# One convolution tap moved from VectorE to ScalarE and GpSimd in a Mamba and FFN block on one core

## The chip, the cores and the metric

The kernel runs on one core of a Trainium2 chip. The metric is the device time of one execution in microseconds; the time before is 591.6 us, the median of three runs (589.13 to 591.79). Besides these there is one profiled execution, from which all views of the profile come.

The names of the engines in the views: PE is TensorE (matmuls; PEld are its weight loads), DVE is VectorE, ACT is ScalarE, POOL is GpSimd, SP is SyncE, which here only issues DMAs.

## The reference

Four sequences of 512 tokens with 256 features go through a Mamba layer and then through an FFN. Both are modulated by a small vector per sequence. Cut to what matters here:

```python
h = _layernorm(x) * (1 + ca) + sa
proj = h @ W_in.T
xBC, z, A_log = split(proj, [CONV_DIM, CONV_DIM + D_INNER])    # 4352, 256, 32 columns
xc = conv_general_dilated(xBC, conv_w, padding=(3, 0), groups=CONV_DIM)
xBC = xc + conv_b                       # causal, 4 taps, each channel for itself
x, B, C = split(xBC, [256, 256 + 2048])  # 32 heads: x 8 wide, B and C 64 wide
a = -softplus(A_log)
Lm = exp(segsum(a))                     # decay from token s to token l, per head
y = (C @ B.T * Lm) @ x + D * x          # per head
x = x + ga * (y * silu(z + z_bias) @ W_out.T)
h = _layernorm(x) * (1 + cb) + sb
x = x + gb * (fwht(silu(h @ W1.T) * (h @ W3.T)) @ W2.T)
```

A channel's convolution is out[l] = b + w3 v[l] + w2 v[l-1] + w1 v[l-2] + w0 v[l-3], where v is a projected channel along the tokens.

## The kernel before

Channels or tokens lie on the 128 partitions, 512 tokens along the free dimension. A sequence is cut into eight chunks of 64 tokens: within a chunk, heads attend by matmuls (`attend`, `intra`); from chunk to chunk, states are handed on (`states`, `turn_states`, `inter`).

**Steps.** The Mamba layer is done in 64 steps k (`NP = 64`), eight for each of eight units n, a unit being half of the heads (i) of one sequence (b). Step k projects 128 channels of B (`bc`, half 0) and 128 of C (`cc`, half 1) with six matmuls each into one PSUM bank (`project`, `proj`, L244), and convolves each (`conv`). Each unit also projects and convolves 128 channels of x (`x_proj`). That makes 64 + 64 + 8 convolutions.

**A convolution** (`conv`, L387 to L394): ACT writes the tap w3 with the bias to `dst` and, in a second pass over the bank, w0 times the bank to a buffer `cv` of three; DVE adds tap w2 (L392) and tap w1 (L393), both read from the bank; POOL, which does not touch the bank, adds `cv`, shifted by three tokens (L394). The framework orders the accesses of different engines to a bank in the order in which the program states them. Three banks (`ps_p`) take turns for the projections.

**Around it.** `attend(k)`, for odd k, multiplies bc and cc of k - 1 and k in 128 small matmuls and weights the results by the decays `lt` (L460, DVE). `turn_b` turns bc with PE and copies it with ACT (L468). A unit's decays from chunk to chunk are made by `x_decays`: ACT takes the exponential of `de` into `dx` (L489), DVE sets the first column to zero (L491), and ACT spreads it eightfold to `dc` (L493), 1024 columns, which the scans over the chunks read in `turn_states` (L561). `turn_states` ends with a masked copy by POOL (`sts`, L565). `x_part2` copies the convolved x twice side by side into `xd`, in two halves of 256 tokens (L507, ACT); `x_part3` turns them with PE (L515) and spreads them for the later matmuls. `xd` and the scans' result `sn` share one pair of buffers (tag "xd").

**Order.** The order of the instructions of each engine is fixed when the program is built. The steps are put in an agenda, and each piece of work is called at its due time, counted in steps: `project` at k - 1.11 and k - 1, `prep_l` at k - 1.31, `attend` at k + 0.12, `x_proj` at 8n + 1.32, `x_part1` (which calls `x_decays`) at 8n + 2.12, `x_part2` at 8n + 3.46, `x_part3` at 8n + 3.77; `turn_states(m)` at 4m + 5.47, two for each unit. A planner with an estimate of every instruction's duration then takes, for each engine but SP, what is ready, by that priority. SP's DMAs stay in the order of the agenda, and each waits on SP until its data and its buffer are there; those behind it wait too. `load_d` at 4m - 3.13 fetches decays for `prep_l`, `x_fetch` at 8n - 1.5 (1.2 for n = 0) fetches `ex` and `de`, `write_sums` writes what they read, and `load_x`, `refill`, `fetch` and the spills move activations and weights. From step 60 on the FFN of the finished sequences begins (`ffn_up`, `ffn_down`).

Of the kernel before, what the change touches and what calls it, by code (L numbers as in the profile page):

```python
# [16 lines left out]
AF = mybir.ActivationFunctionType  # L17
ALU = mybir.AluOpType
# [3 lines left out]
NB, S, DM = 4, 512, 256  # L22
NH, HD = 32, 8
Q = 64
NC = S // Q
# [5 lines left out]
def mamba_ffn(tc, ctx, u, c_t, wmod, win_t, cw, cb, zb, dsk, wo_t, w13_t, w2_t,  # L31
              k_ident, k_reset, k_dl, k_dr, k_had, k_own, out):
    nc = tc.nc
    ve, ac, gp, pe = nc.vector, nc.scalar, nc.gpsimd, nc.tensor
# [14 lines left out]
    def at_time(t, fn, *args):  # L49
        heappush(agenda, (t, next(ids), fn, args))  # L50
# [9 lines left out]
    def work(shape, name, tag, bufs=2, dtype=F32):  # L60
        return wk.tile(shape, dtype, name=name, tag=tag, bufs=bufs)
# [4 lines left out]
    def ptile(name):  # L66
        return ps_p.tile([128, S], F32, name=name, tag="p")
# [174 lines left out]
    def proj(ps, w, c0, ht):  # L242
        for n, (a, b, k) in enumerate(TERMS):
            last[pe] = pe.matmul(ps, w[:, a, k, c0 : c0 + 128], ht[k][:, b], start=(n == 0), stop=(n == 5))  # L244

    last = {}
# [137 lines left out]
            nc.sync.dma_start(p_dr[b][:, 128 * t : 128 * t + 128], phs[32 * t : 32 * t + 32])  # L384
            nc.sync.dma_start(p_end[b][:, 2 * t : 2 * t + 2], phs[32 * t : 32 * t + 32, Q - 1 :: Q])

    def conv(ps, tl, dst):  # L387
        w = cw_sb[:, tl]
        ac.activation(dst, ps, AF.Identity, bias=cb_sb[:, tl : tl + 1], scale=w[:, 3:4])  # L389
        v = work([128, S], "cv", "cv", 3)  # L390
        last[ac] = ac.activation(v, ps, AF.Copy, scale=w[:, 0:1])  # L391
        ve.scalar_tensor_tensor(dst[:, 1:], ps[:, : S - 1], w[:, 2:3], dst[:, 1:], ALU.mult, ALU.add)  # L392
        last["conv"] = ve.scalar_tensor_tensor(dst[:, 2:], ps[:, : S - 2], w[:, 1:2], dst[:, 2:], ALU.mult, ALU.add)  # L393
        last[gp] = gp.tensor_tensor(dst[:, 3:], dst[:, 3:], v[:, : S - 3], ALU.add)  # L394

    units = [(i, b) for i in range(2) for b in range(NB)]
    NP = 64
# [3 lines left out]
    T = dict(  # L401
        attend=0.12, turn_b=0.13, prep_l=-1.31, proj_b=-1.11, proj_c=-1, load_d=-3.13,
        states=-0.03, intra=0.1, turn=1.47, inter=2.53,
        x_proj=1.32, x0=-1.5, x1=2.12, x2=3.46, x3=3.77, gate_z=5.89, fin0=3.54, fin1=3.96, fin2=4.99, fin3=6.63,
        pro0=-11.83, pro1=-7.06, pro2=-4.93, pro3=-4.48, pro4=-3.88, next_ht=-3.77, pro04=0.27,
        quads=1.55, xz1=32.3, wo=19.68, mod=18.99, w2=40.89, wf0=56.74, wf1=62.02, wf2=62.29,
        load_w2=63.01, w2tag=1, w2gp=0, p3gp=1, first_h2=59.14, lag=4.89, next_h2=-2.27,
    )

    def where(k):  # L410
        i, b = units[k // 8]
        return i, b, (k // 4) % 2, k % 4
# [21 lines left out]
    def project(k, half):  # L434
        i, b, pp, g = where(k)
        w = wq[2 * i + pp]
        tl = 2 + 8 * (2 * i + pp) + 2 * g
        dct, nm, nb = ((bcs, "bc", 3), (ccs, "cc", 8))[half]
        pb = ptile(f"p{nm}{k}")
        proj(pb, w, 256 * g + 128 * half, ht[i, b])  # L440
        dct[k] = work([128, S], f"{nm}{k}", nm, nb)
        conv(pb, tl + half, dct[k])

    def attend(k):

# [33 lines left out]
    def x_part1(n):  # L479

        with behind(ac):
            x_decays(n)

    def x_decays(n):
        ex = exs[n]
        ac.activation(ex, ex, AF.Exp)

        de = work([128, 16, NC], f"dx{n}", "dx", 1)
        ac.activation(de.rearrange("p (a g j) c -> p a g (j c)", a=2, g=4),  # L489
                      des.pop(n).rearrange("p (g a j) c -> p a g (j c)", a=2, g=4), AF.Exp)  # L490
        ve.memset(de[:, :, 0:1], 0.0)  # L491
        dc = dcs[n] = work([128, 16, HD, NC], f"dc{n}", "dc", 1)
        ac.activation(dc, de.unsqueeze(2).to_broadcast([128, 16, HD, NC]), AF.Copy)  # L493

    def x_proj(n):
        i, b = units[n]
        px = ptile(f"px{n}")
        proj(px, wxz[i], 0, ht[i, b])
        xcs[n] = work([128, S], f"xc{n}", "xc")
        conv(px, i, xcs[n])  # L500

    def x_part2(n):
        xds[n] = []
        for hf in range(2):
            xd = work([128, 4, 2, Q], f"xd{n}{hf}", "xd", 2)
            xch = xcs[n][:, 256 * hf : 256 * hf + 256].rearrange("p (c l) -> p c l", l=Q)
            ac.activation(xd, xch.unsqueeze(2).to_broadcast([128, 4, 2, Q]), AF.Copy)  # L507
            xds[n].append(xd)

    def x_part3(n):  # L510
# [162 lines left out]
    for k in range(AHEAD):  # L673
        for half in range(2):
            with behind(pe, ve):
                project(k, half)
        if k == 1:
            with behind(gp, ac):
                split_quad(1, 0, q10)
# [46 lines left out]
    hid, pds, x2, gb = {}, {}, {}, {}  # L726
# [48 lines left out]
    for k in range(NP):  # L775
        if k % 2:
            at_time(k + T["attend"], attend, k)
        at_time(k + T["turn_b"], turn_b, k)
        if k >= AHEAD:
            at_time(k + T["proj_b"], project, k, 0)  # L780
            at_time(k + T["proj_c"], project, k, 1)
        if k >= LOOK_P:
            at_time(k + T["prep_l"], prep_l, k)
    for n, (i, b) in enumerate(units):
        if n:
            at_time(8 * n + T["x_proj"], x_proj, n)
        at_time(8 * n + T["x0"] if n else 1.2, x_fetch, n)
        if i == 0 and n > 1:
            at_time(8 * n + T["pro0"] - 2.5, preload, b)
        at_time(8 * n + T["x1"], x_part1, n)  # L790
        at_time(8 * n + T["x2"], x_part2, n)
        at_time(8 * n + T["x3"], x_part3, n)
        at_time(8 * n + T["gate_z"], gate_z, n)
        for part in range(4):
            at_time(8 * n + 8 + T[f"fin{part}"], finish_unit, n, part)
        if n and i == 0:
            for part in range(5):
                at_time(8 * n + T[f"pro{part}"], prologue, b, part)
        if i == 1:
            at_time(8 * n + T["next_ht"], next_ht, b)  # L800
# [89 lines left out]
```

## Time and profile before

| what | us |
|---|---|
| median of the runs | 591.6 |
| the profiled execution | 590.94 |
| its span, from first to last instruction | 588.7 |
| PE busy | 543.6 (92% of the span) |
| PE weight loads busy | 433.2 (74%) |
| DVE busy | 405.1 (69%) |
| ACT busy | 390.5 (66%) |
| POOL busy | 328.0 (56%) |
| POOL's L394, 64 of bc and 64 of cc | 70.1 + 69.8 |
| DVE's L392 and L393 of bc and cc | 47.5 + 47.5 + 47.6 + 47.4 |
| ACT's L389 and L391 of bc and cc | 50.1 + 50.2 + 44.3 + 44.1 |
| ACT's L507, 16 copies to `xd` | 10.3 |
| ACT's L493, 8 copies to `dc` | 8.7 |
| packets of the SP queue: share of 16 DMA engines | 27.2% |

A row of the page's groups reads: line, engine, operation, out<-in by the program's names, shapes, count, then busy us in all and the mean ns of one, then the engine's idle time just before them and what ended most of it. A row of waits reads: who waited, for whom, us in total, how many times, the longest. The span is less than the time of the execution by what lies around the instructions. The busy time of an engine is an average over two stages, the Mamba layer and the FFN, in which different engines are loaded, so the stages have to be looked at apart.

### The profile page before, as it was taken

To read this page: it belongs to the slowest core of one execution; us is meant where nothing else is said; L and a number is where in the kernel's file an instruction comes from. 1 tells how busy PE (TensorE), PEld (TensorE's weight loads), DVE (VectorE), ACT (ScalarE), POOL (GpSimd) and SP (SyncE) were. 2 spreads that over 40 slices of the span, in tenths; PEclk is the share of its full clock that TensorE was granted. 3 is DMA by queue.
4 is the path that set the end of the run, shared out by engine and by line. 5 is a ranking of instruction groups with operands and counts; after the bars stand their busy time and mean duration, and the time that the engine had idled before them with its cause. 6 is when DMAs were issued, how large, how long until landed. Compare 5 with 4: busy or idle time off the path is not lost.

```text
span 588.7 us, 16269 instructions
## 1 busy us (share of the span) xinstructions
PE 543.6 (92%) x6836; PEld 433.2 (74%) x6836; DVE 405.1 (69%) x683; ACT 390.5 (66%) x654; POOL 328.0 (56%) x301
## 2 busy tenths in 40 slices
PE   3698999899899999999999999889989999999996
PEld 3566786677677766777776767667767898888886
DVE  5967878988876776889786878687855454343243
ACT  6889789798965978887795776768674243232321
POOL 5673447445553578466465556467666655334341
PEclk9998999999998999999999899999989999999999
DMA  6423201123012353015003142154148036204021
GB/s 192 124 77 137 70 2 73 26 55 108 18 32 87 114 149 115 3 61 171 7 4 112 76 131 83 60 157 162 37 145 296 2 117 183 77 0 153 1 80 37
DMA packets 42112, 52.00 MB, mean 88 GB/s; under 512 B 18230, under 2 KB 30260, under 8 KB 42040
## 3 DMA queue, kind: packets, MB, share of 16 engines
q1 hardware_dynamic: 40504, 50.54, 27.2%
q8 instruction: 54, 0.88, 0.6%
q10 hardware_dynamic: 1472, 0.38, 0.3%
q14 instruction: 18, 0.15, 0.1%
q0 software_dynamic: 64, 0.05, 0.0%
HBM read 33.51 MB, written 17.44 MB: 87 GB/s over the span
## 4 chain that ended last, share of the span: by engine, by line
PE 40%; DVE 5%; DMA 3%; ACT 2%; issue 2%; POOL 2%; POOLq 0%; DVEq 0%
PE f L244 15%; PE pdy L712 4%; PE pdyi L712 4%; PE pcc L244 4%; PE pbc L244 3%; PE po L612 2%; DMA w2a<-w_t 2%; PE pG L257 1%; PE py L548 1%; PE pi L574 1%; PE bT L466 1%; PE ps L532 1%; DVE sn L561 1%; DMA wf<-w_t 1%; PE px L244 1%
## 5 line engine op out<-in xcount | busy, mean ns | idle before, releaser
L394 POOL TENSOR_TENSOR bc<-bc,cv 128x509 f32<-128x509 f32 x64 | 70.1, 1095 | 58.6 <-DVE bc L393 41.0
L394 POOL TENSOR_TENSOR cc<-cc,cv 128x509 f32<-128x509 f32 x64 | 69.8, 1091 | 56.5 <-DVE cc L393 40.3
L244 PE MATMUL f<-h,wf 128*128 128x512 f32 x384 | 97.6, 395 | 0.0
L244 PEld LDWEIGHTS f<-h,wf 128*128 128x128 f32 x384 | 69.2, 190 | 12.4
L705 POOL TENSOR_TENSOR fl<-ft,fh 128x512 fp32r<-128x512 f32 x31 | 40.1, 1295 | 56.8 <-ACT fh L704 52.0
L392 DVE SCALAR_TENSOR_TENSOR cc<-pcc,cw_sb,cc 128x511 f32<-128x511 f32 x64 | 47.5, 743 | 28.9 <-ACT cv L391 28.9
L389 ACT ACTIVATE bc<-pbc,cb_sb,cw_sb 128x512 f32<-128x512 f32 x64 | 50.1, 783 | 22.8 <-PE pG L257 15.7
L389 ACT ACTIVATE cc<-pcc,cb_sb,cw_sb 128x512 f32<-128x512 f32 x64 | 50.2, 785 | 21.2 <-PE pcc L244 15.6
L244 PE MATMUL pcc<-ht,wq 128*128 128x512 f32 x192 | 53.6, 412 | 6.6 <-DVE dx L491 3.0
L704 ACT ACTIVATE fh<-ft 128x512 fp32r<-128x512 f32 x32 | 20.2, 631 | 58.5 <-DVE ft L701 29.5
L700 DVE SCALAR_TENSOR_TENSOR ft<-ft,f 128x512 f32<-128x512 f32 x32 | 21.9, 687 | 51.5 <-ACT ft L699 49.3
L244 PE MATMUL pcc<-hr,wq 128*128 128x512 f32 x192 | 53.9, 414 | 2.8 <-DVE bc L393 1.9
L392 DVE SCALAR_TENSOR_TENSOR bc<-pbc,cw_sb,bc 128x511 f32<-128x511 f32 x64 | 47.5, 742 | 11.1 <-ACT cv L391 11.0
L244 PE MATMUL pbc<-ht,wq 128*128 128x512 f32 x192 | 54.1, 417 | 0.0
L244 PE MATMUL pbc<-hr,wq 128*128 128x512 f32 x192 | 52.2, 405 | 1.9 <-DVE cc L393 1.8
L393 DVE SCALAR_TENSOR_TENSOR bc<-pbc,cw_sb,bc 128x510 f32<-128x510 f32 x64 | 47.6, 743 | 1.4
L393 DVE SCALAR_TENSOR_TENSOR cc<-pcc,cw_sb,cc 128x510 f32<-128x510 f32 x64 | 47.4, 741 | 1.1
L244 PEld LDWEIGHTS pcc<-ht,wq 128*128 128x128 f32 x192 | 35.5, 193 | 16.4 <-ACT cv L391 3.9
L460 DVE TENSOR_TENSOR l<-pG,l 128x512 f32<-128x512 f32 x64 | 41.0, 681 | 6.7 <-PE pG L257 6.5
L468 ACT ACTIVATE bt<-bT 128x512 f32<-128x512 f32 x64 | 38.8, 606 | 9.9 <-PE bT L466 9.7
L391 ACT ACTIVATE cv<-pbc,cw_sb 128x512 f32<-128x512 f32 x64 | 44.3, 692 | 1.4 <-POOL cc L394 1.4
L391 ACT ACTIVATE cv<-pcc,cw_sb 128x512 f32<-128x512 f32 x64 | 44.1, 690 | 0.0
(152 smaller groups left out, 1231.0 us busy)
## 6 DMA issues: line engine op xcount, KB each, us to landing
wq<-win_t SPq DMA_DIRECT2D x16, 256.0 KB
htd<-ht SPq DMA_DIRECT2D x8, 512.0 KB
hr<-htd SPq DMA_DIRECT2D x8, 512.0 KB
h2d<-ht SPq DMA_DIRECT2D x8, 512.0 KB
h<-h2d SPq DMA_DIRECT2D x8, 512.0 KB
x<-u SPq DMA_DIRECT2D x7, 512.0 KB
ex<-pd SPq DMA_DIRECT2D x8, 256.0 KB
ygd<-yg SPq DMA_DIRECT2D x4, 512.0 KB
```

Of the source, the lines that this page charges most:

```text
L244: last[pe] = pe.matmul(ps, w[:, a, k, c0 : c0 + 128], ht[k][:, b], start=(n == 0), stop=(n == 5))
L389: ac.activation(dst, ps, AF.Identity, bias=cb_sb[:, tl : tl + 1], scale=w[:, 3:4])
L391: last[ac] = ac.activation(v, ps, AF.Copy, scale=w[:, 0:1])
L392: ve.scalar_tensor_tensor(dst[:, 1:], ps[:, : S - 1], w[:, 2:3], dst[:, 1:], ALU.mult, ALU.add)
L393: last["conv"] = ve.scalar_tensor_tensor(dst[:, 2:], ps[:, : S - 2], w[:, 1:2], dst[:, 2:], ALU.mult, ALU.add)
L394: last[gp] = gp.tensor_tensor(dst[:, 3:], dst[:, 3:], v[:, : S - 3], ALU.add)
L460: ve.tensor_tensor(lts[n], pg, lts[n], ALU.mult)
L468: ac.activation(bts[k], pt, AF.Copy)
L700: ve.scalar_tensor_tensor(t, t, 1.0, p1, ALU.add, ALU.mult)
L704: ac.activation(hi, t, AF.Copy)
L705: (ve if (b, f) == (NB - 1, 7) else gp).tensor_tensor(lo, t, hi.bitcast(F32), ALU.subtract)
L712: last[pe] = pe.matmul(pds[t // 2][:, t % 2], hid[a][:, tok], w2h[f][:, w_], start=(f == 0 and t % 2 == 0 and m == 0), stop=(f == 7 and m ...
```

## The change

Five edits:

- For even k, the convolution of `cc` is `shared`: DVE makes only tap w2. ACT makes a third pass over the bank, w1 times the bank to a new buffer `cv1` of two. POOL adds `cv`, shifted by one, to `cv1`, and then adds `cv1`, shifted by two, to `dst`. The other convolutions stay as they are.
- `dc` is spread by POOL.
- `xd` is filled by DMA from SBUF to SBUF, two DMAs for each half of the tokens, four for a unit, all issued by SP.
- `x_part2` is due at 8n + 2.6 in place of 8n + 3.46.
- For n = 0 it is due at 0.6, ahead of `load_d(1)` (0.87), `write_sums` (1.0) and `x_fetch(0)` (1.2).

```diff
-    def conv(ps, tl, dst):
+    def conv(ps, tl, dst, shared=False):
         w = cw_sb[:, tl]
         ac.activation(dst, ps, AF.Identity, bias=cb_sb[:, tl : tl + 1], scale=w[:, 3:4])
         v = work([128, S], "cv", "cv", 3)
         last[ac] = ac.activation(v, ps, AF.Copy, scale=w[:, 0:1])
         ve.scalar_tensor_tensor(dst[:, 1:], ps[:, : S - 1], w[:, 2:3], dst[:, 1:], ALU.mult, ALU.add)
-        last["conv"] = ve.scalar_tensor_tensor(dst[:, 2:], ps[:, : S - 2], w[:, 1:2], dst[:, 2:], ALU.mult, ALU.add)
-        last[gp] = gp.tensor_tensor(dst[:, 3:], dst[:, 3:], v[:, : S - 3], ALU.add)
+        if shared:
+
+            v1 = work([128, S], "cv1", "cv1", 2)
+            ac.activation(v1, ps, AF.Copy, scale=w[:, 1:2])
+            gp.tensor_tensor(v1[:, 1:], v1[:, 1:], v[:, : S - 1], ALU.add)
+            last[gp] = gp.tensor_tensor(dst[:, 2:], dst[:, 2:], v1[:, : S - 2], ALU.add)
+        else:
+            last["conv"] = ve.scalar_tensor_tensor(dst[:, 2:], ps[:, : S - 2], w[:, 1:2], dst[:, 2:], ALU.mult, ALU.add)
+            last[gp] = gp.tensor_tensor(dst[:, 3:], dst[:, 3:], v[:, : S - 3], ALU.add)
...
-        x_proj=1.32, x0=-1.5, x1=2.12, x2=3.46, x3=3.77, gate_z=5.89, fin0=3.54, fin1=3.96, fin2=4.99, fin3=6.63,
+        x_proj=1.32, x0=-1.5, x1=2.12, x2=2.6, x3=3.77, gate_z=5.89, fin0=3.54, fin1=3.96, fin2=4.99, fin3=6.63,
...
-        conv(pb, tl + half, dct[k])
+        conv(pb, tl + half, dct[k], k % 2 == 0 and half == 1)
...
-        ac.activation(dc, de.unsqueeze(2).to_broadcast([128, 16, HD, NC]), AF.Copy)
+        gp.tensor_copy(dc, de.unsqueeze(2).to_broadcast([128, 16, HD, NC]))
...
-            ac.activation(xd, xch.unsqueeze(2).to_broadcast([128, 4, 2, Q]), AF.Copy)
+            for r in range(2):
+                nc.sync.dma_start(xd[:, :, r], xch)
...
-        at_time(8 * n + T["x2"], x_part2, n)
+        at_time(8 * n + (T["x2"] if n else 0.6), x_part2, n)
```

## The prediction

> **What bounds the kernel now.** I read the page's busy table and slices first, then the windows, then the waits of TensorE (PE) inside the window that matters, then single stretches of the timeline. The mamba stage fills about 30 to 440 us, the FFN stage the rest. The windows view of these two (length; then busy us of PE, PEld, DVE, ACT, POOL):
>
> ```profile
> 30.00:440.00 410.00, 383.91 (x5745) 294.21 (x5745) 321.94 (x542) 322.36 (x548) 242.15 (x222) 0.98 0.26 81
> 440.00:588.00 148.00, 143.38 (x1018) 125.74 (x1016) 60.92 (x98) 46.07 (x76) 67.19 (x55) 1.00 0.29 96
> ```
>
> The reader is to see that in the first stage no engine is saturated: PE is busy 94%, VectorE (DVE) and ScalarE (ACT) 79% each, GpSimd (POOL) 59%. The convolutions lie wholly in that stage. PE's idle time there is 410 - 383.9 = 26.1 us. Some time is lost inside its busy time too; the page's groups show it:
>
> ```profile
> L244 PE MATMUL f<-h,wf 128*128 128x512 f32 x384 | 97.6, 395 | 0.0
> L244 PE MATMUL pcc<-ht,wq 128*128 128x512 f32 x192 | 53.6, 412 | 6.6 <-DVE dx L491 3.0
> L244 PE MATMUL pcc<-hr,wq 128*128 128x512 f32 x192 | 53.9, 414 | 2.8 <-DVE bc L393 1.9
> L244 PE MATMUL pbc<-ht,wq 128*128 128x512 f32 x192 | 54.1, 417 | 0.0
> L244 PE MATMUL pbc<-hr,wq 128*128 128x512 f32 x192 | 52.2, 405 | 1.9 <-DVE cc L393 1.8
> ```
>
> The same 512-column matmul costs 97.6/384 = 254 ns in the FFN stage and 213.8/768 = 278 ns in the mamba stage, where the stream is interrupted: 24 ns x 768 = 18.6 us. I count 26.1 + 18.6 = 44.7 us as PE's lost time. The waits view of PE for 30 to 440 us (total, times, longest) says who ended it:
>
> ```profile
> PE pcc L244 <- DVE bc L393: 3.3, 5, 1.2
> PE xt L515 <- DVE l L460: 3.0, 4, 1.2
> PE pcc L244 <- DVE dx L491: 3.0, 3, 2.5
> PE pt L292 <- ACT bt L468: 2.5, 2, 1.6
> PE pcc L244 <- ACT cv L391: 2.2, 2, 1.1
> PE pl L430 <- DMA dr<-p: 2.1, 1, 2.1
> PE pbc L244 <- DVE cc L393: 1.8, 2, 1.2
> PE bT L466 <- ACT bt L468: 1.6, 3, 0.7
> PE pl L430 <- DVE sn L561: 1.3, 2, 0.8
> ```
>
> The rows below these hold 0.2 to 1.2 us each. All rows by releaser: DVE 14.9, ACT 7.5, DMA 2.1, POOL 0.8, together 25.3. So DVE ends 59% of PE's waits, ACT 30%, POOL 3%; laid over 44.7 us that is 26.3, 13.3 and 1.4 us.
>
> **What the Trainium skill says.** "PSUM — Partial Sum Buffer", section "PSUM bank collisions raise a hardware error", says that any two engines on one bank and quadrant must be kept apart, two readers included. The trace agrees: the first DVE tap needs only what L389 wrote, yet it starts after ACT's second read of the same bank (L392 on cc waits for cv L391, 28.9 us in 24 waits). "DMA: Bandwidth & Descriptors", section "Anatomy of one DMA", says that a DMA's semaphore wait happens on the issuing sequencer before dispatch; SyncE (SP) shows this, 80.2 us of waiting at L825 for POOL's ht. "GPSIMD Engine Reference", section "Engine selection", puts POOL at about half of DVE's rate with two inputs and near line rate with one; the two-input add agrees here (1091 ns against 741 ns for the DVE tap of about the same length), the one-input copy isn't shown. "SBUF — State Buffer", section "Who interferes with whom", lets a DVE instruction with two SBUF inputs contend with POOL's reads; the removed tap has one input in PSUM, so no relief of POOL is counted.
>
> **The change part by part.** The page's rows for one conv of cc:
>
> ```profile
> L394 POOL TENSOR_TENSOR cc<-cc,cv 128x509 f32<-128x509 f32 x64 | 69.8, 1091 | 56.5 <-DVE cc L393 40.3
> L393 DVE SCALAR_TENSOR_TENSOR cc<-pcc,cw_sb,cc 128x510 f32<-128x510 f32 x64 | 47.4, 741 | 1.1
> L391 ACT ACTIVATE cv<-pcc,cw_sb 128x512 f32<-128x512 f32 x64 | 44.1, 690 | 0.0
> ```
>
> 1. Taps. The condition holds for even k and half 1: 32 convs of cc. DVE loses 32 x 0.741 = 23.7 us. ACT gains 32 x 0.690 = 22.1. POOL gains one add each, 32 x 1.091 = 34.9; an aligned 512 add takes 1.295 (L705), so at most 32 x 1.295 = 41.4.
>
> 2. dc (L493) leaves ACT, 8 x 1.089 = 8.7 us, for POOL. The trace has no POOL copy. Below, the xpad memset (2048 columns in 1.81 us) gives 0.9 us for 1024; above, a two-input add is about 2.2 ns a column, 2.4 us. I take 1.1, near line rate: 8.8 us. Its reader, the scan L561, comes far later (47.0 to 69.2 us in the first unit), so only POOL's occupancy counts.
>
> 3. xd (L507) leaves ACT, 16 x 0.653 = 10.4 us, for 32 DMAs on SP.
>
> Sums in 30 to 440: DVE 321.9 - 23.7 = 298.2; ACT 322.4 + 22.1 - 8.7 - 10.4 = 325.4; POOL 242.2 + 34.9 + 8.8 = 285.9.
>
> **DVE's relief.** No instruction removed is itself on a tight path: cc of an even k is projected at k - 1 and first read by attend at k + 1.12, two steps of about 6.4 us (410/64) later; so the conv's longer latency (two POOL adds in a row) is free as well. What is gained is a shorter queue in front of DVE. I scale DVE-ended loss with busy over idle: 321.9/88.1 = 3.65 falls to 298.2/111.8 = 2.67, 27% less, 26.3 x 0.27 = -7.1 us. Bounds: 0, if ACT ends the same waits a moment later; -11.9, if half the removed time returns.
>
> **ACT's new wait.** v1 reads the bank after DVE's L392, so by the PSUM rule ACT now waits for DVE, where before it read twice and was done. Queued behind v1 are the next conv's first pass, lt, bt and st, for which PE waits. The mirror wait exists: DVE waited at L392 for ACT 28.9 + 11.0 us over 128 convs, 0.31 us each. Below it is 0; above, a whole L392 and more, 0.75. I take half the mirror, 0.15, since the planner may put other ACT work between: 4.8 us. ACT's effective load 330.2 against 79.8 idle is 4.14, from 322.4/87.6 = 3.68: +12.5%, 13.3 x 0.125 = +1.7 us. At 0 it is +0.6, at 0.31 +2.9, at 0.75 +7.5. The bank comes free at about the same time as before (0.69 for ACT in the place of 0.74 for DVE).
>
> **POOL's load.** 242.2/167.8 = 1.44 becomes 285.9/124.1 = 2.30, +60%: 1.4 x 0.6 = +0.8 us.
>
> **SP's queue.** The 32 DMAs wait on SP for the conv of x and, as xd and sn share two buffers, the second pair for POOL's sts (L565) of the state turned last. Timeline of the fifth unit, start and duration:
>
> ```profile
> 249.91 1.00 POOL L565 TENSOR_TENSOR sts<-sn,own 128x448 f32<-128x448 f32 x1 [0.61 <-DVE dx L491]
> ...
> 252.59 0.67 ACT L507 ACTIVATE xd<-xc 128x512 f32<-128x512 f32 x1
> ...
> 257.75 1.02 PEld L515 LDWEIGHTS xt<-ident,xd 128*128 128x128 f32 x8
> ```
>
> SP issues one DMA in about 0.45 us, and the first dl and dr took about 2.5 us from issue to release PE (25.4 and 25.9 to 28.3). So xd lands near 250.9 + 0.9 + 2.5 = 254.3, and the transposes need it at 257.8: 3.5 us of cover. Behind it on SP wait load_d of the next unit, hr, and in their units quads, w2a and spills. SP ran far ahead there: it issued dl at 227.1 for a prep_l some 8 steps on, and next stood at dr until 248.5. Cost nothing. If the cover goes, each unit pays what it is late, since PE's order is fixed. The 16,384 packets of 256 B add, at the queue's mean 63 ns (27.2% x 16 x 588.7 / 40504), 65 us to each DMA engine, 27 to 38%: hidden.
>
> First unit: x_part2 now stands before load_d(1), the sums' eight DMAs and ex and de. The conv of x ends at 32.9; then come four DMAs (1.8 us), dr (0.4), the sums until about 39, and de 5.8 us after the last of them as before (29.9 to 35.7), near 44.7, landed near 47. ACT used it at 44.1. That is 0 to +3 us; I take 0, as dc isn't read until 69.2 and ACT can do other work first.
>
> **Sum.** 590.94 - 7.1 + 1.7 + 0.8 = 586.3 us, against the profiled execution's 590.94 (span 588.7, 2.2 around it). The median shown is 591.6, so 0.9% faster. About 0.5%, 3 us, is what can be told from no change.
>
> **Rivals.**
> A, forecast: a shorter DVE queue, 586.3, own range 579 to 589. For it: DVE ends 59% of PE's waits. Against: PE is busy 94%.
> B, the gain is eaten: v1 holds ACT 0.6 us each, ACT 344.6/65.4 = 5.27, +43%, +5.7; -7.1 + 5.7 + 0.8 = -0.6, 590.3. For it: DVE and ACT are equally busy, and ACT isn't relieved.
> C, slower, ACT bound to DVE: v1 stands behind L392, which itself stands behind a pair of L460 (1.28) or a scan (1.21). At 1.0 us each ACT is 357.4/52.6 = 6.79, +85%, +11.3: 590.94 - 7.1 + 11.3 + 0.8 = 595.9. It decides from about 0.88 us a wait (+3 us net). Against: L392 mostly follows ACT at once.
> D, slower, late xd: POOL's 18% more work (43.7 on 242.2) delays sts past the 3.5 us of cover; with the transposes 2 us late in each of 8 units it is 586.3 + 16 = 602.3. Against: sts would have to come over 5 us later than now.
>
> **How the numbers follow.** A 0.66, B 0.12, C 0.14, D 0.08. Of A 0.58 lies beyond 0.5% faster and 0.08 within; of B 0.02 faster, 0.07 within, 0.03 slower; C and D slower. Faster 0.60, same 0.15, slower 0.25. The range 577 to 598 leaves out D and the ends of A and C.
>
> **What would show it.** DVE near 381 us in all, ACT near 394, POOL near 372 with a copy of about 1.1 us; PE's DVE-ended waits down by a quarter. C shows as ACT waiting on DVE L392 for over 25 us in total; D as PE xt waiting for a DMA. The forecast is wrong if PE's idle time doesn't fall below 26 us.

## The result, and the profile after

The changed kernel takes 622.9 us (median of 5 runs, 621.6 to 627.4) against 589.7 us for the kernel before (5 runs, the three recorded ahead of the prediction among them). The ratio is 1.0567, interval 1.0528 to 1.0607: 33 us slower, where 4.6 us less was forecast. The profiled span went from 588.7 to 625.3 us.

Where the time went is read first from the windows view. The Mamba stage now fills about 30 to 475 us; these are its first 410 us and the FFN stage (columns as before: length; then busy us of PE, PEld, DVE, ACT, POOL; then TensorE's granted clock, the share of DMA, GB/s):

```profile
30.00:440.00 410.00, 365.82 (x5294) 279.74 (x5293) 288.92 (x473) 303.01 (x520) 263.90 (x241) 0.95 0.28 79
475.00:625.00 150.00, 144.95 (x1072) 126.39 (x1070) 60.94 (x98) 46.28 (x77) 67.30 (x55) 0.99 0.29 94
```

The FFN stage is as it was (145 us of PE in 150, before 143 in 148). In 410 us of the Mamba stage every engine but POOL does less than before: PE 366 us in place of 384. Nobody became the bound; all of them stand more. Over the whole stage (30 to 475 us, before 30 to 440) PE is busy 394.3 us in place of 383.9 and idle 50.7 in place of 26.1. So of the 35 us by which the stage grew, about 25 are standing, and 10 are the same work of PE done more slowly; for these see TensorE's clock below. The groups of the edited convolution show that the moved work itself came out as forecast (line, engine, operation, then busy us and mean ns, idle time before and who ended it):

```profile
L397 POOL TENSOR_TENSOR cv<-cv,cv 128x511 f32<-128x511 f32 x32 | 41.1, 1285 | 39.0 <-ACT cv L396 38.9
L398 POOL TENSOR_TENSOR cc<-cc,cv 128x510 f32<-128x510 f32 x32 | 35.0, 1093 | 0.9
L396 ACT ACTIVATE cv<-pcc,cw_sb 128x512 f32<-128x512 f32 x32 | 22.2, 693 | 15.6 <-DVE cc L392 15.4
L500 POOL COPY dc<-dx 128x1024 f32<-128x1024 f32 x8 | 8.3, 1038 | 5.8 <-DVE dx L498 5.8
```

ACT's third pass is L396, POOL's pair L397 and L398, the spreading of `dc` L500. What is new is in PE's waits, 30 to 475 us (total, times, longest):

```profile
PE py L556 <- DVE xpad L527: 7.4, 3, 5.4
PE xt L523 <- ACT bt L475: 6.3, 2, 5.7
PE pbc L244 <- DVE cc L400: 6.0, 1, 6.0
PE pbc L244 <- ACT cv L396: 5.0, 4, 2.1
```

Before, no wait of PE in this stage was longer than 2.5 us. Now three of 5.4 to 6.0 us stand at 48, 171 and 225 us; all waits of PE in the stage add up to 50.4 us, in place of 25.3 before. At these three, the releasers named are DVE and ACT, but neither was busy: both were standing in front of a DMA. The three places, one by one.

**48 us, the first unit.** SP's timeline of the changed kernel (start, duration, line; x4 are four DMAs in a row):

```profile
33.58 3.74 SPq L515 DMA_DIRECT2D xd<-xc  x4
37.36 0.60 SPq L432 DMA_DIRECT2D dr<-p  x1
...
43.81 0.58 SPq L480 DMA_DIRECT2D ex<-pd  x1
47.61 0.35 SPq L483 DMA_DIRECT2D de<-pend  x1
```

and ACT's timeline, with its idle time before an instruction and who ended it in brackets:

```profile
49.76 0.63 ACT L493 ACTIVATE ex<-ex 128x512 f32<-128x512 f32 x1 [4.96 <-DMA ex<-pd]
52.80 0.31 ACT L496 ACTIVATE dx<-de 128x128 f32<-128x128 f32 x1 [2.42 <-DMA de<-pend]
```

In the kernel before SP issued them earlier:

```profile
32.21 0.54 SPq L473 DMA_DIRECT2D ex<-pd  x1
35.74 0.34 SPq L476 DMA_DIRECT2D de<-pend  x1
```

Now the four `xd` DMAs and the sums stand ahead of them, and `ex` and `de` come 12 us later. ACT reaches its exponentials, cannot go round them, and waits 4.96 + 2.42 us. DVE stands behind ACT for `cc` and PE behind DVE: the 6.0 us of the third row above.

**171 us, the output weights.** SP:

```profile
169.66 2.54 SPq L363 DMA_DIRECT2D p<-parts  x4
172.25 0.59 SPq L206 DMA_DIRECT2D wo<-wo_t  x1
```

DVE:

```profile
174.56 0.29 DVE L207 TENSOR_SCALAR wo<-wo 128x256 f32<-128x256 f32 x1 [3.73 <-DMA wo<-wo_t]
...
175.63 0.69 DVE L527 TENSOR_TENSOR xpad<-xt,own 128x512 f32<-128x512 f32 x1
```

The load of `wo` stands on SP behind DMAs that wait for DVE's `parts` (L358). In DVE's order of the kernel before, the user of `wo` (L207) came some ten instructions after L358 (157.18 us) and found its data:

```profile
162.66 0.28 DVE L207 TENSOR_SCALAR wo<-wo 128x256 f32<-128x256 f32 x1
```

Here only the two of L467 lie between, and it stands ahead of the `xpad` for which PE waits. This stall is therefore not the `xd` DMAs' doing: the last of them had left SP by 160.2 us, nine us before the `parts` were ready, and DVE's order is what changed.

**225 us, the weights of state (2,0).** SP:

```profile
213.12 5.67 SPq L515 DMA_DIRECT2D xd<-xc  x4
...
220.02 0.91 SPq L165 DMA_DIRECT2D wq<-win_t  x2
```

ACT:

```profile
225.77 0.63 ACT L174 ACTIVATE wq<-wq 128x512 fp32r<-128x512 f32 x1 [3.03 <-DMA wq<-win_t]
```

Before, the `wq` loads went out early:

```profile
194.14 0.84 SPq L165 DMA_DIRECT2D wq<-win_t  x2
```

Now SP stands at the `xd` DMAs until 218.8 us, the loads follow at 220.0, and ACT waits for them, 3.03 us here and 1.46 us more at its next instruction (L174 again, 227.86 us). The `bt` that PE needs (L475) is the fourth behind that. The waits of SP show what it stood for (total, times, longest):

```profile
SPq L515 <- ACT xc L389: 67.2, 5, 17.7
...
SPq L515 <- POOL xc L401: 43.2, 8, 11.0
...
SPq L515 <- POOL sts L573: 16.1, 7, 4.3
```

That is 126.5 us of standing at the `xd` DMAs alone. The Trainium skill, "DMA: Bandwidth & Descriptors", section "Anatomy of one DMA — SWDGE (gpsimd) path", says that a DMA's semaphore wait happens on the issuing sequencer. The section is headed for GpSimd's path; these rows show the same for SP, and so everything behind such a DMA waits too. How long SP stands is not yet a price, though: in the run xd below it stands as long at these DMAs (73.5 + 34.8 + 21.1 = 129.4 us), and only 4 us are lost.

**TensorE's clock.** A stall costs more than its own length. The windows around the one at 171 us (the number behind POOL's is the granted clock):

```profile
166.00:171.00 5.00, 3.84 (x81) 2.79 (x79) 4.77 (x7) 4.12 (x7) 2.90 (x3) 1.00 0.06 18
171.00:176.00 5.00, 0.00 (x0) 0.00 (x0) 1.44 (x4) 1.86 (x4) 0.15 (x1) 0.75 0.19 45
176.00:180.00 4.00, 3.63 (x53) 2.93 (x54) 4.00 (x9) 0.63 (x2) 2.89 (x3) 0.50 0.21 49
180.00:190.00 10.00, 10.00 (x158) 8.64 (x158) 5.47 (x12) 5.83 (x11) 5.23 (x5) 0.98 0.47 134
```

From 173.5 us, 2.5 us after PE came to stand, the granted clock is 0.5 for 6.8 us, so PE also does its first 4 us of work after the stall at half clock. It is the same at 48 us (0.5 from 50.6 us) and at 225 us (from 228.1 us), again for 6.8 us each. At clock 0.5 the 512-column matmuls of this run (L244) start 427 ns apart, otherwise 231 ns (medians). In this stage PE works 37.8 us at half clock, in the kernel before 13.3 us. As an estimate from these figures, half of the 24.5 us between them is lost, 12 us, which is near the 10 us of slower work. All seven waits of PE over 2 us in the stage are met or followed at once by such a stretch, as are both of the kernel before; the order in time speaks for the stall as the cause, but no run tests it by itself.

### The profile page after: what moved, and what is told of

Its sections match the earlier page's. It is cut to its first block, busy times and chain, and to the rows that moved or that the text cites. A ratio compares the mean times of both kernels' runs of the same rounds, so it can differ in the third digit from the quotient of the medians.

```text
span 625.3 us, 16343 instructions
## 1 busy us (share of the span) xinstructions
PE 556.2 (89%) x6836; PEld 442.1 (71%) x6836; DVE 391.9 (63%) x651; ACT 393.1 (63%) x662; POOL 374.6 (60%) x341
## 3 DMA queue, kind: packets, MB, share of 16 engines
q1 hardware_dynamic: 57400, 54.73, 29.2%
## 5 line engine op out<-in xcount | busy, mean ns | idle before, releaser
L244 PE MATMUL f<-h,wf 128*128 128x512 f32 x384 | 98.5, 398 | 0.0
L401 POOL TENSOR_TENSOR bc<-bc,cv 128x509 f32<-128x509 f32 x64 | 70.1, 1096 | 43.3 <-DVE bc L400 22.6
L244 PEld LDWEIGHTS f<-h,wf 128*128 128x128 f32 x384 | 69.5, 191 | 12.5
L392 DVE SCALAR_TENSOR_TENSOR cc<-pcc,cw_sb,cc 128x511 f32<-128x511 f32 x64 | 47.6, 744 | 28.5 <-ACT cv L391 28.4
L397 POOL TENSOR_TENSOR cv<-cv,cv 128x511 f32<-128x511 f32 x32 | 41.1, 1285 | 39.0 <-ACT cv L396 38.9
L244 PE MATMUL pbc<-ht,wq 128*128 128x512 f32 x192 | 54.9, 421 | 7.4 <-DVE cc L400 6.0
L392 DVE SCALAR_TENSOR_TENSOR bc<-pbc,cw_sb,bc 128x511 f32<-128x511 f32 x64 | 47.7, 745 | 19.6 <-ACT cv L391 19.5
L244 PE MATMUL pcc<-ht,wq 128*128 128x512 f32 x192 | 55.4, 426 | 3.6 <-DVE bc L400 2.6
L244 PE MATMUL pbc<-hr,wq 128*128 128x512 f32 x192 | 53.9, 416 | 3.7 <-ACT cv L396 3.6
L244 PE MATMUL pcc<-hr,wq 128*128 128x512 f32 x192 | 54.6, 420 | 2.6 <-DVE bc L400 1.6
L467 DVE TENSOR_TENSOR l<-pG,l 128x512 f32<-128x512 f32 x64 | 41.2, 684 | 17.6 <-PE pG L257 16.1
L244 PEld LDWEIGHTS pbc<-ht,wq 128*128 128x128 f32 x192 | 36.1, 197 | 17.2 <-ACT dx L496 6.4
L244 PEld LDWEIGHTS pcc<-ht,wq 128*128 128x128 f32 x192 | 37.7, 203 | 13.6 <-issue 2.1
L473 PE MATMUL bT<-ident,bc 128*128 128x128 f32 x256 | 42.1, 288 | 5.3 <-ACT bt L475 2.8
L244 PEld LDWEIGHTS pcc<-hr,wq 128*128 128x128 f32 x192 | 36.2, 198 | 13.4 <-DVE bc L400 3.6
L257 PEld LDWEIGHTS pG<-cc,bc 64*64 64x64 f32 x2048 | 35.2, 137 | 13.6 <-issue 8.9
```

The lines of the kernel that those rows point to most:

```text
L257: self.before = pe.matmul(*args, **kw)
L397: gp.tensor_tensor(v1[:, 1:], v1[:, 1:], v[:, : S - 1], ALU.add)
L467: ve.tensor_tensor(lts[n], pg, lts[n], ALU.mult)
L473: pe.transpose(pt[:, t], bc[:, 128 * t : 128 * t + 128], ident)
```

## The experiments

Two theories from the start. **SP-queue theory**: the `xd` DMAs hold up the loads behind them on SP, and the in-order engines stand for these. **Lost-order theory**: any edit makes the planner lay out another order of the instructions, and the new order is worse, whatever the edit's work is worth. Ratios are against the kernel before, run in the same session.

Whether an edit changed an engine's order can be read from the traces, by comparing its sequence of instructions by name: what cannot be fitted into the longest common sequence has moved. Between the kernel before and the changed one, 471 of PE's 6836 matmuls have moved.

To see where in the run a kernel loses, I use one mark: the start of the first `xt` transposes of each of the eight units, in PE's records, less that of the kernel before (us):

```
unit           0     1     2     3     4     5     6     7
before      55.6 106.2 156.7 209.9 258.0 303.5 361.3 416.9
after       +8.8  +9.1 +11.9 +14.6 +22.4 +24.4 +26.8 +32.6
n0          +2.3  +3.3  +5.2  +7.4 +13.5 +15.5 +18.4 +24.6
a_wo        +6.4  +6.7  +9.2  +6.2 +13.6 +15.6 +16.7 +20.5
a_quad      +6.5  +7.4  +9.3 +13.5 +13.3 +15.2 +15.7 +15.8
loads       +1.7  +2.0  +4.0  +1.6  +1.8  +3.4  +5.3  +4.4
xd          +5.3  +5.5  +7.6  +4.8  +6.3  +6.2  +5.8  +5.8
xd_gp       +0.9  +4.4 +10.8 +13.9 +17.0 +24.3 +24.5 +28.3
nudge_z     +0.1  +6.4 +11.7 +10.8 +10.2 +10.3  +7.8  +7.1
```

### One part of the change at a time

Run taps: the kernel before with the `conv` of the change and its call alone.

```diff
+            ac.activation(v1, ps, AF.Copy, scale=w[:, 1:2])
+            gp.tensor_tensor(v1[:, 1:], v1[:, 1:], v[:, : S - 1], ALU.add)
+            last[gp] = gp.tensor_tensor(dst[:, 2:], dst[:, 2:], v1[:, : S - 2], ALU.add)
```

> Only the shared taps: xd and dc stay on ACT, x_part2 at 3.46. SP-queue theory (the loss comes from the 32 xd DMAs that hold back other loads on SP): no loss here, -6 to +3 us against before, and ACT's waits on DVE L392 well under 25 us. ACT-wait theory (v1 stands behind L392): +10 us or more, with PE waiting for ACT.

Measured: 599.3 us, ratio 1.0150 (1.0122 to 1.0177).

Run dc: the kernel before with `dc` by POOL alone.

```diff
-        ac.activation(dc, de.unsqueeze(2).to_broadcast([128, 16, HD, NC]), AF.Copy)
+        gp.tensor_copy(dc, de.unsqueeze(2).to_broadcast([128, 16, HD, NC]))
```

> Only the spread of dc by POOL in the place of ACT. SP-queue theory: within 2 us of before. POOL-load theory (POOL's extra work delays sts and the convs): +3 us or more.

Measured: 598.6 us, ratio 1.0143 (1.0104 to 1.0183).

Run xd: the kernel before with the `xd` DMAs and the due times 2.6 and 0.6.

```diff
-            ac.activation(xd, xch.unsqueeze(2).to_broadcast([128, 4, 2, Q]), AF.Copy)
+            for r in range(2):
+                nc.sync.dma_start(xd[:, :, r], xch)
```

> Only xd by DMA, with x_part2 at 2.6 and at 0.6 for the first unit; the convs and dc as before. SP-queue theory: +20 to +36 us, nearly the whole loss, with PE stalls of 5 to 6 us in the first, third and fourth unit behind ex and de, wo and wq. ACT-wait and POOL-load theories: within 3 us of before.

Measured: 594.6 us, ratio 1.0071 (1.0046 to 1.0095); +5.3 us stand at the first unit, and nothing is added later. That is far from the 20 to 36 us that the SP-queue theory expected of these DMAs alone, and taps and dc, of which it expected nothing, lose more than xd. So all three runs miss what it said. In xd the `wq` loads stand behind the `xd` DMAs too, and ACT waits 2.9 us for them, yet the mark moves by 1.5 us there and by 7.8 us in the changed kernel: the late load is dear only together with the other parts. Each part loses by itself, `dc` too, which only takes 8.7 us from ACT; and 8.7 + 8.1 + 4.0 = 20.8 us is not the whole 33. The single parts do not name the cause.

### Does a changed order alone cost?

Run due: the kernel before with the change's two due times for `x_part2` and no other edit. Run nudge_z: the kernel before with one due time moved by a tenth of a step. The edit of due:

```diff
-        x_proj=1.32, x0=-1.5, x1=2.12, x2=3.46, x3=3.77, gate_z=5.89, fin0=3.54, fin1=3.96, fin2=4.99, fin3=6.63,
+        x_proj=1.32, x0=-1.5, x1=2.12, x2=2.6, x3=3.77, gate_z=5.89, fin0=3.54, fin1=3.96, fin2=4.99, fin3=6.63,
...
-        at_time(8 * n + T["x2"], x_part2, n)
+        at_time(8 * n + (T["x2"] if n else 0.6), x_part2, n)
```

and of nudge_z:

```diff
-        x_proj=1.32, x0=-1.5, x1=2.12, x2=3.46, x3=3.77, gate_z=5.89, fin0=3.54, fin1=3.96, fin2=4.99, fin3=6.63,
+        x_proj=1.32, x0=-1.5, x1=2.12, x2=3.46, x3=3.77, gate_z=5.79, fin0=3.54, fin1=3.96, fin2=4.99, fin3=6.63,
```

> The kernel before with nothing but the due times of x_part2 changed (2.6, and 0.6 for the first unit); xd stays on ACT, no instruction is added or taken away. Lost-order theory (any edit makes the planner lay out another order, and the due times fit only the old one): +3 to +10 us. Queue and load theories: within 3 us of before, since no queue holds anything new.

> The kernel before with gate_z due at 5.79 in the place of 5.89: the same instructions, the same order on SP, another order on the compute engines. Lost-order theory: slower by 3 us or more. Queue and load theories: within 2 us of before.

Measured: due 589.9 us, ratio 1.0002 (0.9983 to 1.0022). nudge_z 597.8 us, ratio 1.0155 (1.0088 to 1.0222), with the same instructions as the kernel before, SP's order the same, and 300 of PE's 6836 matmuls moved. In due the order of every engine, SP too, is exactly that of the kernel before; so this run is a repeat of it, and says nothing about the lost-order theory. nudge_z does: an edit without any work can lose 1.5% (0.9 to 2.2%). A loss of that size in one run of one part, taps or dc (147 and 407 of PE's matmuls moved), cannot be put down to the part's work. The 5.7% of the whole change is far beyond it; whether an order can cost so much was not tested.

### The loads behind xd

Run n0: the changed kernel with the first unit's `xd` DMAs behind `load_d(1)`, the sums, `ex` and `de`.

```diff
-        at_time(8 * n + (T["x2"] if n else 0.6), x_part2, n)
+        at_time(8 * n + (T["x2"] if n else 1.25), x_part2, n)
```

> The changed kernel, but the first unit's x_part2 due at 1.25, behind load_d(1), the sums and x_fetch(0). SP-queue theory: the stall of 6 us at 48 us goes, 6 to 9 us less than the changed kernel, the rest of the loss stays. ACT-wait theory: as the changed kernel within 3 us.

Measured: 617.7 us, ratio 1.0457 (1.0414 to 1.0500). The stall at 48 us is gone and the first unit's +8.8 us falls to +2.3; the later ones stay. This is the cleanest test of all: the order of PE, DVE, ACT and POOL is that of the changed kernel, instruction by instruction, and only SP's differs. So the 1.1%, 6.5 us, is the price of what stood behind these four DMAs, `ex` and `de` first of all.

Run loads: n0's edit, and two loads earlier, that of `wo` and those of the state (2,0) (due before at 28.55).

```diff
-        quads=1.55, xz1=32.3, wo=19.68, mod=18.99, w2=40.89, wf0=56.74, wf1=62.02, wf2=62.29,
+        quads=1.55, xz1=32.3, wo=17.6, mod=18.99, w2=40.89, wf0=56.74, wf1=62.02, wf2=62.29,
...
+    early_q = []
+    def early_fetch():
+        early_q.append(fetch_quad(2, 0))
...
-        at_time(t + T["quads"], load_quad, n, half)
+        if (n, half) == (2, 0):
+            at_time(26.5, early_fetch)
+            at_time(t + T["quads"], lambda: split_quad(2, 0, early_q.pop()))
+        else:
+            at_time(t + T["quads"], load_quad, n, half)
```

> The changed kernel with three loads put ahead of the xd DMAs on SP: the first unit's sums, ex and de (x_part2(0) at 1.25), wo (17.6) and the first half of the first weights of the second half of the heads (fetched at 26.5, split when it was). SP-queue theory: the three PE stalls of 5.4 to 6.0 us go, 12 to 18 us less than the changed kernel. Lost-order theory: other stalls come in their place, less than 8 us gained.

Measured: 595.3 us, ratio 1.0112 (1.0084 to 1.0139). All the moved work is still there, taps, `dc` and `xd`; three loads stand ahead of the DMAs they had stood behind, and 4.55% of the 5.67% are gone, 27 us. The deviation stays between 1.6 and 5.3 us (row loads of the table), no stall over 5 us is left, and PE works 12.6 us at half clock in place of 37.8. PE's order is about as far from that of the kernel before (443 matmuls moved) as the changed kernel's (471), so an order so far off need not cost more than 1.1%. In this run ACT's exponential of `ex` starts at 44.35 us without a wait.

Runs a_wo and a_quad: the changed kernel with one of the two early loads each (the edits are those of loads).

> The changed kernel with one edit: wo due at 17.6 instead of 19.68. SP-queue theory: the stall at 171 to 176 us (DVE 3.7 us for wo, PE 5.4 us for xpad) goes, and with it the growth from +11.9 to +14.6 us at the fourth unit: 615 to 620 us; the stalls at 46 and 225 us stay. If the three loads add up, their shares of 27.6 us are about 5 (first unit), 4 to 6 (wo) and the rest (quad). Lost-order theory: 614 to 631 us without relation to that stall.

> The changed kernel with one edit: the four wq loads of the state (2,0) issued at 26.5 instead of 28.55, splits unmoved. SP-queue theory: the stall at 225 to 231 us (ACT waits 3.0 us for wq, PE 5.75 us for bt) goes; by the transposes of the fifth unit, which move there from +14.6 to +22.4 us, 6 to 10 us are won: 612 to 617 us. Lost-order theory: 614 to 631 us without relation to that stall.

Measured: a_wo 613.1 us, ratio 1.0403 (1.0346 to 1.0461); a_quad 606.3 us, 1.0289 (1.0236 to 1.0342). Both won more than expected, 1.64% and 2.78%. In the table each takes its step out where its load is: a_wo has +9.2 and then +6.2 us where the change has +11.9 and +14.6; a_quad stays at +13.3 where the change jumps to +22.4. With n0's 1.10% the three make 5.5%, or 33 us; together in loads they made 27. Of a_quad's gain 9 us are there at unit 4; the rest comes in units 6 and 7, where nothing was edited, and its cause is not shown. Unlike n0, both edits also move instructions of the computing engines (79 and 150 of PE's matmuls), and nudge_z moved the marks by steps of 5 to 6 us with 300. That the steps vanish where they were expected to speaks for the loads; how much of each gain is order is not shown.

Run b_loads, the control: the two early loads in the kernel before, and nothing of the change.

> The kernel before, with two of the three early loads of the run loads and nothing of the change: wo due at 17.6 instead of 19.68, and the four wq loads of the state (2,0) issued at 26.5 with their splits left at 28.55. (The first x_part2 of the kernel before is due at 3.46 and holds nothing up.) SP-queue theory: before has no wait of over 2 us for either load, so issuing them earlier is worth nothing by itself: 587 to 593 us, and the 27 us that loads took back were the delay that the change had made, not a gain of their own. Rival, that early loads would have sped up any version: 580 us or less. Lost-order theory: up to 599 us, since the order of the computing engines is laid out anew.

Measured: 587.7 us, ratio 0.9963 (0.9946 to 0.9980). By themselves the early loads are worth 0.4%, not 4.5%. What loads took back was the delay that the change had made. This version is also the fastest complete one measured: 0.4% below the kernel before, 5.7% below the changed kernel.

Run xd_gp: the changed kernel with the `xd` DMAs issued by POOL.

```diff
-                nc.sync.dma_start(xd[:, :, r], xch)
+                gp.dma_start(xd[:, :, r], xch)
```

> The changed kernel with the 32 xd DMAs issued by POOL in the place of SP, so that SP's queue is that of the kernel before but for its order in time. SP-queue theory: 12 to 20 us less than the changed kernel, although POOL issues 32 DMAs of about 0.65 us each, 21 us. POOL-load theory: slower than the changed kernel.

Measured: 620.3 us, ratio 1.0532 (1.0470 to 1.0594): the expected gain did not come. Like the runs of single parts, this one speaks against the SP-queue theory as a full account. ACT's waits for `ex`, `de` and `wq` fell from 11.9 to 1.4 us, and the first unit is whole again (+0.9 us); the stall for `wo` stayed (DVE 3.7 us), as it hangs on `parts` and not on `xd`. But the deviation still grows to +28 us by the last unit, through seven waits of PE of 2 to 4 us, all for DVE or ACT. 13.8 us of PE's waits end with ACT's third pass (L396), in place of 5.3 in the changed kernel. POOL does not stand at the DMAs (0.3 us of waiting), yet it issues them, about 0.78 us each: 25 us more in front of its adds. And its order is quite another: 601 of PE's matmuls moved against the changed kernel. Which of these took the gain back is open. For late loads on SP as the cause speak n0, loads, a_wo and a_quad, each of which takes out the loss where its load is. For the `xd` DMAs as what makes them late speak only n0 and a_quad: the stall for `wo` is there in dc, which has no `xd` DMA, and here, where SP issues none.

### What the relief of VectorE is worth

The other half of the forecast: 23.7 us less for DVE, worth 7.1 us. Run drop leaves the 32 taps out and gives them to no engine (`cc` lacks that tap there), the most that relief can bring; b_drop does so on b_loads.

```diff
-        last["conv"] = ve.scalar_tensor_tensor(dst[:, 2:], ps[:, : S - 2], w[:, 1:2], dst[:, 2:], ALU.mult, ALU.add)
+        if not shared:
+            last["conv"] = ve.scalar_tensor_tensor(dst[:, 2:], ps[:, : S - 2], w[:, 1:2], dst[:, 2:], ALU.mult, ALU.add)
```

> The kernel before with VectorE's second tap left out in the 32 convolutions that the change shares, and given to no engine (that tap is missing from the output's cc). 23.7 us less of VectorE and nothing more elsewhere: the most that relief of VectorE can bring. The prediction's step (7.1 us, bounds 0 to 11.9): 582.4 us, 578 to 590. Rival, VectorE's queue is no bound because the next releaser is as late: within 3 us of before, 587 to 593. Lost-order theory: slower by up to 10 us although work is only taken away.

> The same leaving out of 32 taps, on b_loads (587.7 us: wo due at 17.6, wq loads of the state (2,0) issued at 26.5). Prediction's step: 580.6 us, 576 to 588. Rival, no bound: 585 to 591. Lost-order theory: slower than b_loads by up to 10 us; if drop and b_drop differ from their bases by more than 5 us in unlike directions, the order decides and not VectorE's work.

Measured: drop 586.7 us, ratio 0.9979 (0.9957 to 1.0001); b_drop 586.6 us, 0.9973 (0.9950 to 0.9996), against 0.9963 for b_loads. That is 1.2 us at the first base and nothing at the second, though work was only taken away. PE's waits that DVE ends, 30 to 440 us, went from 14.9 to 14.1 us in drop, by a twentieth and not by 27%. The relief was worth 7 us in neither run. Their order is not quite that of their bases (116 and 109 of PE's matmuls moved), so a small gain hidden by order is not excluded.

Runs b_taps, b_tact and b_tpool: on b_loads, the whole shared tap, and on b_drop its two halves alone: ACT's pass (POOL adds `v1` in place of `v`, so the tap of `v` is missing), and POOL's extra add (of `v` with itself, shifted, so `cc` has other values). The lines of the 32 convolutions in b_tact:

```diff
+            ac.activation(v1, ps, AF.Copy, scale=w[:, 1:2])
+            last[gp] = gp.tensor_tensor(dst[:, 2:], dst[:, 2:], v1[:, : S - 2], ALU.add)
```

and in b_tpool:

```diff
+            gp.tensor_tensor(v1[:, 1:], v[:, 1:], v[:, : S - 1], ALU.add)
+            last[gp] = gp.tensor_tensor(dst[:, 3:], dst[:, 3:], v1[:, 1 : S - 2], ALU.add)
```

> b_loads with the 32 shared taps (ScalarE and GpSimd take them), xd and dc left on ScalarE. If the taps' +8.7 us in the single run was mainly loads that came late in a new order, it is nearly gone here: 586 to 591 us. If the taps' work on ScalarE costs: 595 to 598 us, and ScalarE's waits on VectorE's first tap are well above the 15.4 us of the changed kernel. Prediction's step: 583 us.

> b_drop with ScalarE's part of the shared taps alone: the second pass v1 is written in the 32 convolutions, and GpSimd adds v1 in place of v, one add as before (the tap of v is missing from cc there). Rival C of the prediction in its mild form, ScalarE's pass and its wait for VectorE cost: 593 to 597 us, and ScalarE waits 10 to 15 us for VectorE's first tap. The prediction's step (+1.7 us): 586 to 590. GpSimd theory: as the prediction's step.

> b_drop with GpSimd's part alone: one more two-input add in each of the 32 convolutions, of v with itself shifted (cc gets other values there), and ScalarE no more than before. GpSimd theory, its adds hold VectorE's short operations in the chain of dt and the decays: VectorE's operations of lines 349 to 370 grow from 0.3 to over 1 us where an add runs beside them, and the time is 592 to 597 us. ScalarE theory and the prediction's step (+0.8 us): 586 to 590.

Measured: b_taps 597.0 us, ratio 1.0149 (1.0098 to 1.0200); b_tact 593.0 us, 1.0048 (1.0016 to 1.0079); b_tpool 588.2 us, 0.9969 (0.9946 to 0.9992). POOL's add alone costs nothing over b_drop. With ACT's pass alone 0.75%, 4.4 us, are lost, and the trace agrees: all waits of PE, 30 to 440 us, are 26.1 us in place of b_drop's 21.4. ACT waits there 12.1 us for DVE's L392. But 0.75% is less than nudge_z lost without any work, and 133 of PE's matmuls moved here, so how much of it is the pass is not settled. Both together cost 1.76%, 10.4 us, more than the sum. Of the rest the trace of b_taps shows a part. DVE's timeline:

```profile
106.03 1.14 DVE L355 CAST parts<-phs 128x128 bf16<-128x128 f32 x1
107.09 1.37 DVE L370 TENSOR_TENSOR df<-phs 128x128 f32<-128x128 f32 x1
108.39 1.17 DVE L356 TENSOR_TENSOR rest<-phs,parts 128x128 f32<-128x128 f32 x1
```

and POOL's, the same moments:

```profile
105.79 1.29 POOL L397 TENSOR_TENSOR cv<-cv,cv 128x511 f32<-128x511 f32 x1 [1.27 <-ACT cv L396]
107.05 1.27 POOL L608 TENSOR_TENSOR yg<-xc,yg 128x512 fp32r<-128x512 f32 x1
108.28 1.13 POOL L398 TENSOR_TENSOR cc<-cc,cv 128x510 f32<-128x510 f32 x1
```

Each DVE instruction begins inside an instruction of POOL and ends within 0.2 us of its end. Their means in b_loads are 0.23, 0.28 and 0.28 us: 2.9 us are lost here. In b_loads POOL hits the two instructions ahead of them instead (L349 and L351, 0.88 and 1.40 us at this place, 0.29 and 0.42 here, 1.6 us), so the chain from L349 to L356 is 1.4 us longer in b_taps (4.39 against 2.97 us), and it starts later, since it waits for ACT's exponentials (L348). Then comes `l` (L467), for which PE waits at the transposes at 107.8 and again at 161.3 us, 3.0 us each. In b_loads these two waits are 1.2 us, in b_tact, without POOL's second add, 1.9 us, and in b_tpool 0.2 us. So the halves meet: ACT's pass shifts the chain, and POOL's adds lengthen it.

### Two more combinations

Run loads_nt: loads without the shared taps (the call of `conv` as before). Run b_dc: b_loads with `dc` by POOL (the edit of dc).

> The run loads (595.3 us) without the shared taps: dc by POOL, xd by DMA and the three early loads stay. DVE gets back 32 taps of 0.74 us, ACT loses 32 passes of 0.69 us, POOL loses 32 adds. If the shared taps are worth what the prediction took (7.1 us less through DVE's queue, less 1.7 through ACT's and 0.8 through POOL's), this is slower than loads: 599 to 601 us. If they cost, as the single run of the taps said (+8.7 us), it is faster: 586 to 591 us. Lost-order theory: within 3 us of loads or off by up to 9 us either way, with PE's stalls elsewhere.

> b_loads with the chunks' decays spread by GpSimd, all else as in b_loads. If the loss of the single run dc was the late wo load (VectorE 3.6 us, PE 4.8 us at 164 to 170 us) and what follows from it, it is gone: 584 to 589 us, with 8.7 us less for ScalarE. Lost-order theory: up to 598 us with PE's stalls elsewhere.

Measured: loads_nt 593.2 us, ratio 1.0077 (1.0053 to 1.0101), so the taps do not help when the loads are in time: with them it is 1.0112. At all three bases, the kernel before, b_loads and this one, the version with the taps is the slower, at this one by no more than the intervals leave open. b_dc 596.2 us, ratio 1.0142 (1.0090 to 1.0194). The stall for `wo` that the run dc had (DVE 3.6 us, PE 4.8 us) is gone in b_dc, and the loss is the same as in dc (against its own base b_loads even 1.8%), so that stall was not its cause. The profiled execution, span 590.4 us, is the fastest of its four (592.4 us, the others 595.2 to 598.6) and had a granted clock of 0.994, before 0.985, so it shows little of the loss. Its order is far from its base's: 443 of PE's matmuls moved, more than in nudge_z. And loads_nt, which contains the same edit and the `xd` DMAs as well, loses only half as much. So order is a candidate; why `dc` by POOL alone costs 1.4% stays open.

## Why the prediction was wrong, point by point

**The sums** were nearly right, for the engines' busy times. ACT 393.1 us (394 forecast), POOL 374.6 (372), POOL's copy 1.04 us (1.1), POOL's first add 1.285 us, near the upper end of its bounds. DVE came to 391.9 us where 381 was forecast; about 8 of the 10 us are short instructions that became longer beside POOL's work (below). The share of the SP queue's packets came to 29.2% where up to 38% was priced; that they stay hidden was right. One reading was too kind: the prediction lets the two-input add agree with "about half of DVE's rate", but 741 ns against 1091 is two thirds of it; the forecast used the measured figure.

**The step that failed is "SP's queue", with its "Cost nothing".** It asked whether `xd` itself would land in time for PE's transposes, and there it was right: PE never waited for a DMA at `xt`, and rival D, which priced only this, did not come. What stands behind the 32 DMAs was listed ("load_d of the next unit, hr, and in their units quads, w2a and spills") and put at nothing, on the reason that SP ran far ahead. But the `xd` DMAs wait for freshly made data and take that lead away: the `wq` loads (quads) went out 26 us later than before, ACT and PE stood for them, and issuing them early won 2.8%, the dearest single term. `wo`, 1.6%, was not in the list and is no matter of `xd`: there, DVE's new order brought the user of a load forward.

**"First unit … 0 to +3; I take 0"** failed on its reason, "ACT can do other work first". ACT's order is fixed when the program is built. The `de` load went out at 47.6 and not at 44.7 us, mainly because the four `xd` DMAs held SP for 3.7 us and not 1.8, and ACT had it at 52.8, 5.2 us after its issue where 2.3 were taken. Nothing needed `dc` before 69 us, but ACT stood in front of `ex` and `dx` all the same, and with it the convolution of the next step. It cost 8.8 us at the first unit, 5 to 6.5 in the end by n0, whose order of the computing engines is unchanged.

**"DVE's relief", -7.1 us**, was mis-sized. Taking all the work away for nothing brought 1.2 us or none (drop, b_drop), near the lower bound given, 0. Scaling waits by busy over idle failed: 7% less work left PE's waits for DVE where they were (14.1 us in place of 14.9). The reason that the prediction gave for its bound, that ACT ends the same waits a moment later, was not tested.

**"ACT's new wait", +1.7 us**, was probably too small: b_tact lost 4.4 us, order included, inside the bounds given (0.6 to 7.5). A wait was 12.1/32 = 0.38 us there and 15.4/32 = 0.48 in the changed kernel, where 0.15 was taken. Rival C's waits are there, at less than half of the 1.0 us each that it took; its sign of 25 us was not reached. **"POOL's load", +0.8 us**, is nothing by itself (b_tpool), but not beside ACT's pass (b_taps).

**What no step held:** that a forecast by durations assumes the old order. nudge_z shows 1.5% for no work at all, and the change moved more of PE's order than that run did (471 matmuls, 300 there). Nor did any step hold that PE works on at half clock after a stall, by the estimate above about 12 us here. The forecast's own test, PE's idle time falling below 26 us, failed: in the same 410 us it is 410 - 365.8 = 44 us.

Of the 33 us, then, moving three loads ahead takes back 27; in n0, a_wo and a_quad each does so at its own place. Shown free of any other change are the 6.5 us of n0; in the other two, order has a share that is not known. And xd shows that these DMAs alone, without the taps and `dc`, cost only 4 us. For the remaining 6 to 7 us of loads, the taps' ACT pass is a candidate; how much of it is order is not settled.

## What to carry to other kernels

Before a copy is moved from an engine to a DMA queue, list every DMA behind it on that queue, find the first user of each on its engine, and ask what that engine does next: an in-order engine stands in front of late data even when nobody needs the result yet. If the DMA must wait for freshly computed data, put the loads that need no data ahead of it. Where a build-time planner sets the order, measure what a meaningless nudge costs before a single edit's per cent is read as its worth, and compare the orders in the traces: an edit that leaves them alone, as n0 did, is the one that can be read.

## What the runs showed of the hardware

- Short DVE instructions with both inputs in SBUF, and casts, stretch to the end of the POOL instruction beside them: in b_taps from 0.28 to 1.37 us (L370) and from 0.23 to 1.14 us (L355). In the changed kernel 28 DVE instructions are over 0.2 us longer than the shortest of their line, names and shape, 22.6 us in all; 26 of them end within 0.3 us after an instruction of POOL does. Before it was 21 and 14.8 us. DVE's taps, whose first input is in PSUM, stay at 0.74 us. The Trainium skill, "SBUF — State Buffer", section "Who interferes with whom", agrees: the ports that DVE and GpSimd share are an exclusive lock, a DVE instruction with two SBUF inputs contends with a GpSimd instruction that reads SBUF, and a cast can contend in its two-port modes. The prediction cited it for POOL's side alone; it works on DVE's side too, and in the taps' versions POOL's adds meet the chain of `phs` and `parts`.
- Four `xd` DMAs from SBUF to SBUF held SP for 3.7 us in the first unit (33.58 to 37.32), 0.94 us each, where 0.45 had been taken from other DMAs; on POOL two took 1.58 us.
- POOL's two-input add took 1.285 us for 511 columns and 1.093 us for 510.
- After PE stood for 2.5 to 3 us in the three long stalls, the clock that TensorE was granted fell to 0.5 for 6.8 us each. The mean over the changed kernel's profile was 0.961, before 0.985. In the 143 runs of the kernel before in the sessions of the experiments, the 15 with a mean clock of 0.978 to 0.980 took 591.3 us on average, and the 15 above 0.9895 took 586.6 us.
